# Text softmax of a cross-attention layer: exponentials taken per head from PSUM, with the row sums alongside

## The chip, the core and the metric

The kernel runs on one core of a Trainium2 chip. A core has TensorE (PE, matrix products, with its weight loads PEld), VectorE (DVE), ScalarE (ACT), GpSimd (POOL) and SyncE (SP, which issues DMAs here). Each engine works through its own queue in order; semaphores tie the queues together. Working data lie in SBUF; TensorE writes to eight PSUM banks, from which VectorE and ScalarE read. The metric is the device time of one execution in microseconds, the median of several runs.

## The reference, cut to what matters

Two batches, 2048 image tokens of width 640, 128 context tokens of width 384, of which the last four are adapter tokens; 8 heads of 80. "The text" is the attention over the first 124 context tokens:

```python
query = hidden_states @ Wq
keyt = enc @ Wk          # 124 text tokens
valt = enc @ Wv
hs = _mha(query, keyt, valt)
# _mha, per head:
scores = einsum('bhqd,bhkd->bhqk', qh, kh) * d ** -0.5
probs = softmax(scores, axis=-1)
out = einsum('bhqk,bhkd->bhqd', probs, vh)
# adapter part: ca_q1 from the four adapter tokens attends over all of hidden_states,
# its result, through Wq, attends over the four tokens -> ca_hs2
out = (hs + ca_hs2) @ Wout + b_out + residual
```

All is float32.

## The kernel before

The program is written out by hand for TensorE: every matmul and transposition is recorded in the order in which the Python generators yield it, and TensorE keeps that order. VectorE, ScalarE and GpSimd take what the recording layer gives them, in order too; `dve.behind` adds order on VectorE without a wait. Line 28 is the helper through which all matmuls go, line 41 that of the transpositions, line 55 that of all VectorE instructions.

**The text.** `scores(m)` (line 971) works on unit m, two tiles of 128 query rows. For each tile and each half u of four heads, six matmuls put 4 x 124 scores into one PSUM bank `sc` (128 x 496). VectorE takes the maximum of each head (`m`, 128 x 4, line 993) and writes scores less maximum into the SBUF tile `e` (in the profile `p`, lines 994 to 997), which ends the bank's use. When both halves are there, one ScalarE instruction takes the exponential of all 8 heads in place (line 999, 128 x 992). `divided` (line 1007) sums each head on VectorE (`r`, line 1012), takes the reciprocal, and has GpSimd multiply the probabilities by it (line 1014); it is called one tile later. `turned_out` (line 1031) transposes both tiles in 32 x 32 blocks on VectorE (`eb`) and sends them to HBM (`kept`); `turned` (line 1017) reads them back as `pT`; `values` (line 1056) multiplies them by the values (`ph`), copies the result to SBUF (`hsT`, by ScalarE or VectorE in turn), multiplies by the output weights (`po`) and adds the residual rows `xo` on VectorE. The pool of `e` has two buffers, that of `m` and `r` three.

**The adapter.** `maxima` (line 792) computes scores `s` of the adapter's queries against image rows, four banks at a time, and has VectorE take their maxima (`mx`, 128 x 2048). `contraction` (line 825) computes them again row by row: four matmuls write `s` (the four banks of `q4`, one buffer), ScalarE takes the exponential into `ea` (line 856, 128 x 1536), and the products with it are accumulated in `acc`. In TensorE's order the scores of step st+1 stand behind the products of step st-1 and a stretch of text work, and they need the four banks that `ea` of step st has read. At the end of each half `accs` (line 863) is copied by ScalarE.

**The order.** `weave` and `Mix` lay the text between the steps of the adapter: first all of batch 0's maxima, beside them the queries `pq`; then batch 0's contraction (in the profile from about 154 to 290 us) with text units 0 to 4; batch 1's maxima (to about 462 us) with units 5 to 8; batch 1's contraction (to about 592 us) with units 9 to 11; and then the rest of the text alone. Until then four of the eight banks belong to the adapter's scores and one to its accumulation (batch 1's maxima lend that one out), so that the text, the queries and the outputs share three or four; after that all eight.

Of the kernel before, what the change touches and what calls it, by code (L numbers as in the profile page):

```python
# [8 lines left out]
F32 = mybir.dt.float32  # L9
AF = mybir.ActivationFunctionType  # L10
ALU = mybir.AluOpType
AX = mybir.AxisListType

P = 128
HEADS = 8
# [4 lines left out]
class TensorInOrder:  # L20
# [6 lines left out]
    def matmul(self, out, lhsT, rhs, **kw):  # L27
        ins = self.tc.nc.tensor.matmul(out, lhsT, rhs, **kw)  # L28
        self.tc.keep_in_program_order(ins)
        n = 1  # L30
        for size in rhs.shape[1:]:
            n *= size
        if min(lhsT.shape[0], lhsT.shape[1]) <= 32:
            self.us += (n / 1.2 + 97) / 2e3
        elif min(lhsT.shape[0], lhsT.shape[1]) <= 64:
            self.us += (n / 1.2 + 54) / 1e3
        else:
            self.us += 2 * max(n / 1.2, 109) / 1e3
# [139 lines left out]
def kernel(  # L178
# [39 lines left out]
    nc = tc.nc  # L218
    pe = TensorInOrder(tc)
    dve = VectorBehind(tc)  # L220
    B, S, H = x.shape
    NTOK, CAD = enc.shape[1], enc.shape[2]
    NK = NTOK - T
# [6 lines left out]
    SCALE = float(D) ** -0.5  # L230
# [28 lines left out]
    def mm_tile(name, pool=None):  # L259
        if pool is None:  # L260
            pool = ps_turns[ps_turn[0] % len(ps_turns)]
            ps_turn[0] += 1
        return pool.tile([P, 512], F32, tag="mm", name=name)
# [72 lines left out]
    small = ctx.enter_context(tc.tile_pool(name="small", bufs=3))  # L336
# [629 lines left out]
    def tiles(m):  # L966

        b, m = divmod(m, NST // 2)
        return [(b, 2 * m + k) for k in range(2)]

    def scores(m):

        q = q_of[m // 2]
        before = None
        for b, st in tiles(m):
            rows = slice(st % 4 * P, (st % 4 + 1) * P)
            e = pools["e"].tile([P, HEADS, NTOK], F32, tag="e", name=f"p_{b}_{st}")
            for u in range(2):
                sc = mm_tile(f"sc_{b}_{st}_{u}")
                for i, c in enumerate((2 * u, 2 * u + 1, 4)):  # L980
                    to = sc[:, : 4 * NK].rearrange("p (i j k) -> p i j k", i=2, j=2)
                    n0 = 2 * c if c < 4 else 2 * (4 + u)
                    matmul(
                        to[:, i, :, :] if c < 4 else to[:, :, 1, :],
                        q[:, c, rows],
                        kpad[:, b, n0 : n0 + 2, :],
                        start=(i == 0),
                        stop=(i == 2),
                        skip_group_check=True,
                    )  # L990
                s4 = sc[:, : 4 * NK].rearrange("p (h k) -> p h k", k=NK)
                m = small.tile([P, 4], F32, tag="m", name=f"m_{b}_{st}_{u}")
                dve.tensor_reduce(m, s4, AX.X, ALU.max)
                dve.tensor_tensor(
                    e[:, 4 * u : 4 * u + 4, :NK], s4,
                    m.unsqueeze(2).to_broadcast([P, 4, NK]), ALU.subtract,
                )
                yield
            nc.scalar.activation(e[:, :, :NK], e[:, :, :NK], AF.Exp, scale=SCALE)  # L999
            nc.gpsimd.memset(e[:, :, NK:], 0.0)  # L1000
            if before is not None:
                divided(*before)
            before = b, st, e
        yield
        divided(*before)

    def divided(b, st, e):

        last = dve.last
        et = e[:, :, :NK]  # L1010
        r = small.tile([P, HEADS], F32, tag="r", name=f"r_{b}_{st}")
        dve.behind(dve.tensor_reduce(r, et, AX.X, ALU.add), last)
        dve.reciprocal(r, r)
        nc.gpsimd.tensor_tensor(et, et, r.unsqueeze(2).to_broadcast([P, HEADS, NK]), ALU.mult)  # L1014
        e_of[b, st] = e

# [174 lines left out]
    def ahead(m):  # L1191

        parts, needs, more = [], [], []
        if m + 1 < units:
            more = [turned(m + 1, 1 if m + 2 == units else 3), residual(m + 1)]
        more.append(completed())
        if m + 2 < units:
            parts.append(stage(("s", m + 2), scores(m + 2)))  # L1200
        if m + 3 == units:
            parts.append(out_soon(m + 2))
        n = m // 2 + 2
        if NSB <= n < len(blocks):
            if m % 2 == 0:
                parts.insert(0, room(n))
                parts.append(queries(n, (0, 1, 2)))
                needs += [("again", *blocks[n]), slots.free(1)]
            else:
                parts.append(stage(("q", *blocks[n]), queries(n, (3, 4))))  # L1210
        return stage(("t", m), unit(m, more, parts), *needs)
# [56 lines left out]
    for sb in range(NSB):  # L1268
# [6 lines left out]
    open_late()  # L1275
    first = chain(
        stage(("s", 0), scores(0)),
        together(turned(0, 1), stage(("s", 1), scores(1)), residual(0)),
    )
    text.parts[:] = [beside(first, chain(*text.parts), 2), *[ahead(m) for m in range(units)]]  # L1280
# [68 lines left out]
```

## Time and profile before

| | us |
|---|---|
| median of 3 runs (lowest, highest) | 747.44 (747.37, 749.98) |
| the profiled execution | 744.53 |
| its span, first to last instruction | 742.8 |
| VectorE, row sums `r`, 32 of 1,165 ns | 37.3 |
| VectorE, maxima `m`, 64 of 666 ns | 42.3 |
| GpSimd, products by the reciprocals, 32 of 1,964 ns | 61.2 |

Times in the profile's groups are busy time, mean ns of one instruction, and then the idle time of the engine just ahead of the group, with what ended it. "x64" is the number of instructions. In a timeline the first two columns are start and duration in us, counted from the span's start; the bracket says how long the engine had been idle and what released it. TensorE's granted clock was full (1.00) in every stretch of this execution.

By stage, TensorE was busy for 142.4 of the first 149.9 us, 135.9 of the 140.1 us to 290.0, 170.4 of the 172.0 us to 462.0, 134.0 of the 135.0 us to 597.0 and 142.4 of the last 145.8 us. VectorE was busy for 77, 66, 123, 45 and 65 us of these stretches, ScalarE for 31, 56, 32, 57 and 17 us.

### The profile page before, as it was taken

To read this page: it belongs to the slowest core of one execution; us is meant where nothing else is said; L and a number is where in the kernel's file an instruction comes from. 1 tells how busy PE (TensorE), PEld (TensorE's weight loads), DVE (VectorE), ACT (ScalarE), POOL (GpSimd) and SP (SyncE) were. 2 spreads that over 40 slices of the span, in tenths; PEclk is the share of its full clock that TensorE was granted. 3 is DMA by queue.
4 is the path that set the end of the run, shared out by engine and by line. 5 is a ranking of instruction groups with operands and counts; after the bars stand their busy time and mean duration, and the time that the engine had idled before them with its cause. 6 is when DMAs were issued, how large, how long until landed. Compare 5 with 4: busy or idle time off the path is not lost.

```text
span 742.8 us, 9398 instructions
## 1 busy us (share of the span) xinstructions
PE 725.1 (98%) x3809; PEld 371.3 (50%) x3809; DVE 376.3 (51%) x507; ACT 193.4 (26%) x239; POOL 133.1 (18%) x184
## 2 busy tenths in 40 slices
PE   7999999999989999999999999999999999999998
PEld 4543433343444446555445454444433556566765
DVE  2155746544274537678768585412330546346631
ACT  2221121033444342212021110543434411011100
POOL 7000000002021013225311221010010012631330
PEclk9999999999999999999999999999999999999999
DMA  9927240004734867599988294500910426985793
GB/s 291 176 36 126 34 38 1 0 1 115 106 119 71 200 97 177 133 261 225 226 167 215 36 198 111 147 20 19 190 49 19 136 84 201 232 218 157 213 247 95
DMA packets 147429, 96.28 MB, mean 130 GB/s; under 512 B 118133, under 2 KB 118965, under 8 KB 145338
## 3 DMA queue, kind: packets, MB, share of 16 engines
q1 hardware_dynamic: 142266, 85.10, 48.1%
q0 software_dynamic: 5120, 10.59, 8.1%
q8 instruction: 30, 0.49, 0.3%
q14 instruction: 13, 0.11, 0.1%
HBM read 63.81 MB, written 31.85 MB: 129 GB/s over the span
## 4 chain that ended last, share of the span: by engine, by line
PE 92%; DVE 4%; issue 1%; ACT 1%; DMA 0%; POOL 0%; DVEq 0%; ACTq 0%; POOLq 0%
PE po L28 24%; PE pq L28 24%; PE s L28 13%; PE sc L28 11%; PE acc L28 6%; PE ph L28 5%; PE pyz L28 3%; PE pk L28 1%; PE pv L28 1%; PE pt_y L41 1%; DVE m L55 1%; DVE p L55 1%; ACT ea L856 1%; DVE xt L55 1%; DVE mx L55 0%
## 5 line engine op out<-in xcount | busy, mean ns | idle before, releaser
L28 PE MATMUL po<-wout_sb,hsT 128*128 128x320 f32 x640 | 186.6, 438 | 0.8 <-DVE xo L55 0.6
L28 PEld LDWEIGHTS po<-wout_sb,hsT 128*128 128x128 f32 x640 | 118.4, 190 | 70.1 <-issue 25.1
L28 PE MATMUL pq<-xt,wq_sb 128*128 128x512 f32 x320 | 151.4, 605 | 0.0
L55 DVE TENSOR_REDUCE mx<-s 128x4 f32<-128x2048 f32 x48 | 109.9, 2290 | 65.9 <-PE s L28 65.9
L856 ACT ACTIVATE ea<-s 128x1536 f32<-128x1536 f32 x64 | 92.7, 1448 | 111.4 <-PE s L28 111.3
L1014 POOL TENSOR_TENSOR p<-p,r 128x992 f32<-128x992 f32 x32 | 61.2, 1964 | 263.4 <-DVE r L55 263.3
L55 DVE TENSOR_TENSOR xo<-xo,po 128x320 f32<-128x320 f32 x64 | 30.9, 483 | 141.0 <-PE po L28 140.6
L28 PE MATMUL sc<-kpad,q 128*128 128x248 f32 x384 | 94.1, 384 | 0.9 <-DVE p L55 0.9
L28 PEld LDWEIGHTS pq<-xt,wq_sb 128*128 128x128 f32 x320 | 57.2, 189 | 74.3 <-issue 68.6
L28 PEld LDWEIGHTS sc<-kpad,q 128*128 128x128 f32 x384 | 69.2, 189 | 33.7 <-issue 18.1
L55 DVE TENSOR_REDUCE m<-sc 128x4 f32<-128x496 f32 x64 | 42.3, 666 | 53.8 <-PE sc L28 53.8
L28 PE MATMUL s<-ca,yz 32*128 32x384 f32 x512 | 59.4, 533 | 2.3 <-ACT ea L856 2.3
L272 ACT COPY q<-pq 128x512 f32<-128x512 f32 x29 | 17.0, 585 | 166.0 <-PE pq L28 166.0
L999 ACT ACTIVATE p<-p 128x992 f32<-128x992 f32 x32 | 33.0, 1030 | 93.2 <-DVE p L55 93.2
L28 PE MATMUL s<-yz,ca 32*128 32x512 f32 x384 | 54.7, 640 | 1.8 <-DVE mx L55 1.0
L1109 POOL DMA_INDIRECT xo<-o,query x24 | 37.4, 1557 | 100.3 <-DMA xo<-in_x_dram 50.6
L28 PE MATMUL acc<-ea,y_sb 128*32 128x384 f32 x512 | 54.5, 498 | 0.2 <-ACT ea L856 0.2
L28 PE MATMUL ph<-pT,vpad 128*32 128x256 f32 (+1 forms) x512 | 50.0, 387 | 1.8 <-DVE hsT L55 1.8
L55 DVE TENSOR_TENSOR p<-sc,m 128x496 f32<-128x496 f32 x64 | 42.6, 670 | 1.7
L55 DVE STREAM_TRANSPOSE eb<-p 128x1024 f32<-128x1024 f32 x32 | 38.1, 1222 | 3.6 <-POOL p L1014 3.6
L28 PE MATMUL pq<-xt,wq 128*128 128x512 f32 x80 | 38.3, 603 | 0.0
L55 DVE TENSOR_REDUCE r<-p 128x8 f32<-128x992 f32 (+1 forms) x34 | 37.7, 1111 | 0.0
(142 smaller groups left out, 390.6 us busy)
## 6 DMA issues: line engine op xcount, KB each, us to landing
kept<-eb SPq DMA_DIRECT2D x16, 1024.0 KB, 5.3
pT<-kept SPq DMA_DIRECT2D x64, 256.0 KB, 6.0
xi<-in_x_dram SPq DMA_DIRECT2D x44, 256.0 KB, 5.1
xo<-in_x_dram SPq DMA_DIRECT2D x32, 320.0 KB, 4.8
out_dram<-xo SPq DMA_DIRECT2D x22, 320.0 KB, 3.2
xi<-in_x_dram SPq DMA_DIRECT2D x44, 64.0 KB, 4.7
early<-xo SPq DMA_DIRECT2D x8, 320.0 KB, 2.6
xe<-early SPq DMA_DIRECT2D x8, 320.0 KB, 6.0
```

The source lines that it names most:

```text
L28: ins = self.tc.nc.tensor.matmul(out, lhsT, rhs, **kw)
L41: ins = self.tc.nc.tensor.transpose(out, in_, ident)
L55: self.last = getattr(self.tc.nc.vector, name)(*args, **kw).ins
L272: nc.scalar.copy(dst, src)
L856: nc.scalar.activation(e, q4[:, :, :CAD], AF.Exp, scale=SCALE)
L999: nc.scalar.activation(e[:, :, :NK], e[:, :, :NK], AF.Exp, scale=SCALE)
L1014: nc.gpsimd.tensor_tensor(et, et, r.unsqueeze(2).to_broadcast([P, HEADS, NK]), ALU.mult)
L1109: nc.gpsimd.indirect_dma_start(out=t, out_offset=None, in_=o2_of[b], in_offset=bass.IndirectOffsetOnAxis(ap=query[:, st : st + 1], axis=0) ...
```

## The change

The subtraction of the maxima and the row sums leave VectorE. VectorE multiplies the four maxima of a half by minus the scale, in place (128 x 4). ScalarE then takes the exponentials straight from the PSUM bank, one instruction for each head (128 x 124), with the scaled maximum as its bias and the row's sum as a second output, written into a column of `r`, which is now made in `scores`. The instruction over all heads goes, and so does the row sum in `divided`, which keeps the reciprocal. TensorE's and SyncE's orders stay the same instruction for instruction.

```diff
             e = pools["e"].tile([P, HEADS, NTOK], F32, tag="e", name=f"p_{b}_{st}")
+            r = small.tile([P, HEADS], F32, tag="r", name=f"r_{b}_{st}")
...
                 dve.tensor_reduce(m, s4, AX.X, ALU.max)
-                dve.tensor_tensor(
-                    e[:, 4 * u : 4 * u + 4, :NK], s4,
-                    m.unsqueeze(2).to_broadcast([P, 4, NK]), ALU.subtract,
-                )
+                dve.tensor_scalar(m, m, -SCALE, None, ALU.mult)
+                for i in range(4):
+                    h = 4 * u + i
+                    nc.scalar.activation(
+                        e[:, h, :NK], s4[:, i, :], AF.Exp, bias=m[:, i : i + 1], scale=SCALE,
+                        accum_out=r[:, h : h + 1],
+                    )
                 yield
-            nc.scalar.activation(e[:, :, :NK], e[:, :, :NK], AF.Exp, scale=SCALE)
             nc.gpsimd.memset(e[:, :, NK:], 0.0)
...
-    def divided(b, st, e):
+    def divided(b, st, e, r):
         last = dve.last
+        dve.behind(dve.reciprocal(r, r), last)
         et = e[:, :, :NK]
-        r = small.tile([P, HEADS], F32, tag="r", name=f"r_{b}_{st}")
-        dve.behind(dve.tensor_reduce(r, et, AX.X, ALU.add), last)
-        dve.reciprocal(r, r)
         nc.gpsimd.tensor_tensor(et, et, r.unsqueeze(2).to_broadcast([P, HEADS, NK]), ALU.mult)
```

## The prediction

> **What bounds the kernel now.** I read the busy shares and the chain of waits first, then the groups by form, then the timeline of the two contractions.
>
> ```profile
> PE 725.1 (98%) x3809; PEld 371.3 (50%) x3809; DVE 376.3 (51%) x507; ACT 193.4 (26%) x239; POOL 133.1 (18%) x184
> PE 92%; DVE 4%; issue 1%; ACT 1%; DMA 0%; POOL 0%; DVEq 0%; ACTq 0%; POOLq 0%
> ```
>
> TensorE sets the time: busy for 725.1 of 742.8 us. Of the 17.7 us left, 4.35 pass before its first instruction and about 3 at the end, so no relief of another engine can bring more than some 10 us, and a microsecond by which TensorE waits longer is a microsecond of the result.
>
> ```profile
> L999 ACT ACTIVATE p<-p 128x992 f32<-128x992 f32 x32 | 33.0, 1030 | 93.2 <-DVE p L55 93.2
> L856 ACT ACTIVATE ea<-s 128x1536 f32<-128x1536 f32 x64 | 92.7, 1448 | 111.4 <-PE s L28 111.3
> L775 ACT ACTIVATE yz<-pyz,ones 128x512 f32<-128x512 f32 x16 | 10.1, 683 | 31.9 <-PE pyz L28 31.9
> L272 ACT COPY q<-pq 128x512 f32<-128x512 f32 x29 | 17.0, 585 | 166.0 <-PE pq L28 166.0
> L272 ACT COPY vca<-pvca 128x128 f32<-128x128 f32 x1 | 0.3, 265 | 0.4 <-PE pvca L28 0.4
> L272 ACT COPY vpad<-pv 124x32 f32<-124x32 f32 x8 | 1.1, 199 | 0.0
> L55 DVE TENSOR_TENSOR p<-sc,m 128x496 f32<-128x496 f32 x64 | 42.6, 670 | 1.7
> L55 DVE RECIPROCAL r<-r 128x8 f32<-128x8 f32 x32 | 6.4, 201 | 0.9
> ```
>
> These rows price what goes and what comes. The next, from the timeline of batch 0's contraction, shows where ScalarE reaches TensorE:
>
> ```profile
> 247.35 0.93 PE L28 MATMUL s<-ca,yz 32*128 32x384 f32 x8
> 247.46 0.67 DVE L55 TENSOR_REDUCE m<-sc 128x4 f32<-128x496 f32 x1 [0.73 <-PE sc L28]
> 248.17 0.67 DVE L55 TENSOR_TENSOR p<-sc,m 128x496 f32<-128x496 f32 x1
> 248.94 1.03 ACT L999 ACTIVATE p<-p 128x992 f32<-128x992 f32 x1 [3.19 <-DVE p L55]
> 249.87 1.43 ACT L856 ACTIVATE ea<-s 128x1536 f32<-128x1536 f32 x1
> 251.36 0.93 PE L28 MATMUL s<-ca,yz 32*128 32x384 f32 x8 [1.28 <-ACT ea L856]
> ```
>
> The last sc group ends at 247.35, where s begins. From there a chain runs over the maximum, the subtraction, the text's exponential and, behind it in ScalarE's queue, ea; the next s needs ea's four banks. The chain is 4.01 us long here and TensorE stands idle for 1.28. It existed only for the second half of a tile; behind a first half ea followed s at once. One place of that kind, in batch 1's contraction:
>
> ```profile
> 577.75 2.36 DVE L55 STREAM_TRANSPOSE eb<-p 128x1024 f32<-128x1024 f32 x2
> 578.29 0.93 PE L28 MATMUL s<-ca,yz 32*128 32x384 f32 x8
> 579.34 1.45 ACT L856 ACTIVATE ea<-s 128x1536 f32<-128x1536 f32 x1 [3.36 <-PE s L28]
> 580.03 0.64 DVE L55 TENSOR_REDUCE m<-sc 128x4 f32<-128x496 f32 x1
> 580.94 0.93 PE L28 MATMUL s<-ca,yz 32*128 32x384 f32 x8
> ```
>
> Here VectorE is busy with the transpositions when the scores of 578.29 are ready, the maximum is 1.63 us late (580.03 against 578.40), and nobody cares: ea has not waited for it, and the next s stands 2.65 us behind the last.
>
> **VectorE's side.** It loses 64 subtractions (64 x 0.670 = 42.6 us) and 32 row sums (32 x 1.165 = 37.3 us), and gains 64 small multiplications of 128x4. Nearest row: the reciprocal of 128x8, 0.20 us, so 12.8 us. 67 us less, but VectorE is no bound: the places where TensorE visibly waits for its work, at 213.27 (1.84 us) and 345.94 (0.87), are all that can come back. As bounds for one multiplication I take 0.15 (the reduction of 128x4 to 128x1 at 8.20 us) and 1.83 us: in the first 12 us of the timeline eight multiplications of 128x16 and 128x4, from SBUF to SBUF, show 0.97 to 1.83 us, all of them ending at 11.3 to 11.4 us, while GpSimd runs fills from 9.62 to 11.27.
>
> The Trainium skill has a rule for this, SBUF — State Buffer, section Who interferes with whom: a VectorE instruction in a two-port mode, which a multiplication with all operands in SBUF can enter, and a GpSimd instruction lock each other out for a whole instruction. That rule speaks against the change, since the subtraction it replaces read PSUM. By it each multiplication that meets a GpSimd product would take up to 1.96 us; by the reciprocal's row, 0.20.
>
> I take 0.20: in the contractions GpSimd is busy for only 4.4 of the 80 us from 460, and its products come ahead of the transpositions, not beside the maxima. I charge the long one in the upper bound alone, at 345 us, where a GpSimd gather starts at 345.09 for 1.54 us.
>
> **ScalarE's side.** It loses 32 x 1.030 = 33.0 us and gains 256 exponentials of 128x124 with a bias column and a sum. Without both, a copy of 128x128 out of PSUM takes 0.265 us; the bias column costs 683 - 585 = 0.098; together 0.363. Instructions that follow each other overlap by 0.10 (two y_sb copies of 0.589 last 1.07), so one head adds 0.263. The sum's price stands in no row. Lower bound nothing: it is formed as the elements pass. Upper bound 0.30: if a second small instruction has to deliver it, nearest row the 124x32 copy of 0.199 us, unable to start before the first has drained, so that the 0.10 overlap is lost as well. I take the middle, 0.15: a step of 0.413 (bounds 0.263 and 0.563), 1.65 us for four heads (1.05 to 2.25). ScalarE then carries 193 - 33 + 256 x 0.413 = 266 us, 36%: on average no bound.
>
> The Trainium skill's page ScalarE: Activation LUTs, section What ACT_TABLE_LOAD costs, gives about 280 ns plus 0.833 per element for an ACTIVATE with a bias column and 93 ns of overlap back to back: 290 ns for a head, without the sum; by that figure the four heads would take 1.16 us instead of the 1.05 of the rows. Its fixed price per instruction speaks against cutting one instruction of 992 elements into eight.
>
> **The path.** The new chain from the end of a sc group to the next possible s: 0.11 to the maximum, 0.67, 0.04 gap, 0.20 multiplication, 0.10 to ScalarE, the four heads, 1.43 ea, 0.05 = 2.60 + 1.65 = 4.25 us (3.65; 4.85). The same sum for the old second half (0.67 for the multiplication, 0.94 for the heads) gives the 4.01 seen. What is new is that *both* halves have it. ea is queued behind the heads, and s and the accumulation wait for ea. Going through the two contractions, with the distance from the sc group's end to the next s before (each value: middle; lower; upper):
> - 158.68 to 161.77 (3.09 us): +1.16; 0.56; 1.76. 201.07 to 204.17 (3.10): +1.15; 0.55; 1.75. Behind 180.8 and 191.9 lie 4.41 us: 0; 0; 0.44 each.
> - 204 to 215: the row sums (1.17 and 1.13 us) stood ahead of GpSimd's products, these ahead of the transpositions, and these ahead of the idle 1.84. GpSimd now starts sooner, but its second product waits for the heads, and the next ea behind heads that wait for the transpositions. s of 214.29 comes some 0.8 earlier: -0.84; -1.0; -0.2.
> - 243.24: the maximum is 1.44 late behind eb (244.79); 4.25 + 1.44 against 4.11 = 1.58, of which the following pair with its 1.28 of idle time gives back 0.91: +0.67; -0.3; 1.9.
> - Four halves in a row, 466.25 to 482.43, 3.96 to 4.11 us apart: each second one is late, since a late s also makes the next sc late; less the 0.48 of idle time at 481.9: +0.39; -0.36; 1.6. 527.15 to 534.79: +0.36; -0.3; 1.3.
> - 578.29: 4.25 + 1.63 against 2.65 = +3.23; 2.63; 3.83. The largest single term.
> - 590.26: accs now stands behind four heads, and the transposition at 591.15 waits for it: +0.60; 0; 1.2.
>
> In batch 1's maxima ea doesn't run, but a bank is held until the last head has read it. At 345.94 TensorE waited for the bank of the scores whose subtraction ended at 345.79; the heads end at 345.09 + 0.34 + 1.65 = 347.08: +1.3; 0.7; 1.9, and 1.4 more if the multiplication waits for GpSimd. At 433.12 about +0.3; 0; 1.0. After 597 us eight banks are there and ScalarE is busy for 17 of 146 us: nothing. The last transpositions end at 710.6 and their pT is asked for at 716.7, behind other DMAs of SP's queue; without row sums on VectorE the heads' 3.3 us fit in before that. If they didn't, the last ph group (725.5) would be late. `r` and `m` now live longer, until GpSimd's product and the last head; each has three buffers and at most two are in use at those times, so nothing; with fewer, the maximum of a later half would wait for the heads.
>
> Sum: 1.16 + 1.15 - 0.84 + 0.67 + 0.39 + 0.36 + 3.23 + 0.60 + 1.6 = +8.3 us; lower +2.5; upper +18.3. Against the profiled 744.53: 752.8. The median of the runs lies 2.91 above that execution, so the forecast is 747.44 + 8.3 = 755.7 us.
>
> **The rivals.** (A) The sum is free and the heads overlap fully (0.263 a head): the lower sum, 749.9. For it: ScalarE's rows differ only by elements and bias. Against: a second output has to be written by something. (B) Each head is drained before its sum is written (0.563): 765.7. For it: 256 small outputs; against: no such wait in any row. (C) Faster: relief of VectorE decides. Its place is the idle time behind VectorE and behind ea after a subtraction: 1.84 + 1.28 + 0.87 + 0.48 + 0.48 = 4.95 us, so 742.5. It decides if the heads cost less than subtraction and exponential did, 2.60 + 4 x step below 4.01, with margin, step under 0.25, and if the late maxima at 244.79 and 580.03 did not reach ea. The second condition speaks strongly against it: ScalarE's order puts those heads ahead of ea.
>
> **How the numbers follow.** Forecast (step 0.35 to 0.5) 0.57, A 0.18, B 0.18, C 0.05, something unseen 0.02. The change of this kernel that a measurement can tell from none is about 0.5%, 3.7 us. A falls to both sides of it, mostly within: slower 0.80, same 0.15, faster 0.05. The range leaves out C, the bottom of A and the top of B: 749 to 764.
>
> **What would show it.** Right: rows of 128x124 at 0.36 us with a step near 0.41; ScalarE near 266 us and VectorE near 309; an idle TensorE of about 3 us at the s behind the scores of 578; ea released by text exponentials. Wrong: TensorE's busy share unchanged (A), or idle time at every s of the contractions (B); multiplications of 128x4 well over 0.2 us throughout; a late pT at the end. The step's length is what most decides the size.

## The result, and the profile after

| us | before | after |
|---|---|---|
| median (lowest, highest) | 747.37 (745.29, 749.98), 7 runs | 752.72 (751.90, 753.66), 7 runs |
| the profiled execution | 744.53 | 753.52 |
| its span | 742.8 | 751.8 |
| its mean granted clock | 1.000 | 0.995 |

The ratio is 1.0082 with a 95% interval of 1.0061 to 1.0102: 0.8% slower, 5.35 us between the medians, 3.0 us less than forecast. The first view is again that of the busy shares and of the chain of waits.

```profile
PE 729.1 (97%) x3809; PEld 372.6 (50%) x3809; DVE 308.4 (41%) x475; ACT 251.9 (34%) x719; POOL 133.6 (18%) x184
...
PE 91%; DVE 4%; ACT 3%; issue 1%; DMA 1%; POOL 0%; SPq 0%; DVEq 0%; ACTq 0%
```

VectorE lost 68 us of work and TensorE is still busy for 97% of the span; among the engines' shares of the chain only ScalarE's rose, from 1 to 3%. The groups by form show what VectorE and ScalarE do now:

```profile
L998 ACT ACTIVATE p<-sc,m 128x124 f32<-128x124 f32 x256 | 89.7, 368 | 96.1 <-DVE m L55 89.0 <-PE ph L28 7.1
L998 ACT ACTIVATION_READ_ACCUMULATOR p<-sc,m 128x1 f32 x256 | 53.4, 209 | 0.0
L55 DVE TENSOR_SCALAR m<-m 128x4 f32<-128x4 f32 x64 | 10.6, 167 | 1.7
```

The second output is an instruction of its own, 0.209 us long. What a head really takes is not to be had by adding the two means; it is read from the distance of the starts, in the timeline of the chain that starts at 203.74 us (at 201.07 before the change):

```profile
203.74 0.93 PE L28 MATMUL s<-ca,yz 32*128 32x384 f32 x8
203.85 0.67 DVE L55 TENSOR_REDUCE m<-sc 128x4 f32<-128x496 f32 x1 [0.56 <-PE sc L28]
204.56 0.17 DVE L55 TENSOR_SCALAR m<-m 128x4 f32<-128x4 f32 x1
...
204.84 0.36 ACT L998 ACTIVATE p<-sc,m 128x124 f32<-128x124 f32 x1 [3.41 <-DVE m L55]
205.10 0.19 ACT L998 ACTIVATION_READ_ACCUMULATOR p<-sc,m 128x1 f32 x1
205.20 0.36 ACT L998 ACTIVATE p<-sc,m 128x124 f32<-128x124 f32 x1
...
206.22 1.46 ACT L856 ACTIVATE ea<-s 128x1536 f32<-128x1536 f32 x1
...
207.73 0.93 PE L28 MATMUL s<-ca,yz 32*128 32x384 f32 x8 [0.83 <-ACT ea L856]
```

The read-out starts at 205.10, before the exponential's 0.36 us are over, and the next head at 205.20, before the read-out ends. Four heads take 206.22 - 204.84 = 1.38 us, 0.345 each, and the chain from the scores' end to the next s 207.73 - 203.74 = 3.99 us. The place that the forecast called the largest, after:

```profile
579.95 1.42 PE L28 MATMUL sc<-kpad,q 128*128 128x248 f32 x6
581.29 0.93 PE L28 MATMUL s<-ca,yz 32*128 32x384 f32 x8
...
583.04 0.64 DVE L55 TENSOR_REDUCE m<-sc 128x4 f32<-128x496 f32 x1
...
584.00 0.36 ACT L998 ACTIVATE p<-sc,m 128x124 f32<-128x124 f32 x1 [5.01 <-DVE m L55]
...
585.37 1.46 ACT L856 ACTIVATE ea<-s 128x1536 f32<-128x1536 f32 x1
...
586.88 1.66 PE L28 MATMUL s<-ca,yz 32*128 32x384 f32 x8 [2.87 <-ACT ea L856]
588.48 1.51 PE L28 MATMUL acc<-ea,y_sb 128*32 128x384 f32 x8
```

The maximum is late behind `eb` as before, but now ea stands behind the four heads that wait for it: ea starts at 585.37 instead of at some 582.3 (1.05 behind its s, as before), and TensorE is idle for 2.87 us. Then something happens that no step of the forecast holds: s takes 1.66 us instead of 0.93, and the accumulation 1.51 instead of 0.85. The stretches of 5 us show why (columns: length; busy time and number of instructions of PE, PEld, DVE, ACT and POOL; TensorE's granted clock; DMA share; GB/s):

```profile
580.00:585.00 5.00, 4.02 (x31) 1.85 (x29) 3.70 (x5) 1.00 (x6) 0.25 (x2) 1.00 0.23 95
585.00:590.00 5.00, 3.12 (x17) 0.80 (x17) 0.00 (x0) 3.63 (x7) 0.00 (x0) 0.59 0.78 246
590.00:595.00 5.00, 5.00 (x30) 2.71 (x30) 1.54 (x3) 1.35 (x8) 0.00 (x0) 0.73 0.00 0
```

The missing share, 0.41 x 5 + 0.27 x 5 = 3.4 us, is 6.8 us at half clock, and inside the span the trace's clock records have exactly one such piece, 6.83 us from 585.9 on.

Where the time went is seen when each of the 3809 matmuls is set against itself in the trace of before (their order is the same): the steps of that delay, measured from the first matmul of each.

| place (us before) | forecast: middle (lower; upper) | step in the trace |
|---|---|---|
| first 12 us | not named | +1.4 |
| 153 | not named | +0.61 |
| 158.68 to 161.77 | +1.16 (0.56; 1.76) | +0.88 |
| 201.07 to 204.17 | +1.15 (0.55; 1.75) | +0.90 |
| 204 to 218 | -0.84 (-1.0; -0.2) | -1.91 + 0.82 - 0.22 = -1.31 |
| 243.24 to 251.4 | +0.67 (-0.3; 1.9) | +1.28 - 1.28 = 0 |
| 290 | not named | -0.42 |
| 345.94; 433.12 | +1.3 (0.7; 1.9); +0.3 (0; 1.0) | +1.04; +0.07 |
| 466 to 482 | +0.39 (-0.36; 1.6) | +0.03 |
| 527 to 535 | +0.36 (-0.3; 1.3) | +0.35 - 0.32 = +0.03 |
| 578.29 | +3.23 (2.63; 3.83) | +2.94 |
| half clock behind it | not named | +2.7 |
| 590 | +0.60 (0; 1.2) | +0.34 |
| sum | +8.3 | +9.25 |

The sum is that of the two profiled executions (spans 9.0 apart, the first matmul 0.25 earlier; smaller steps elsewhere are not listed). Without the start, 7.85; without the half clock too, 5.1.

### The profile page after: what moved, and what is told of

Read it like the earlier page. It is cut to its first block, busy times and chain, and to the rows that moved or that the text cites. A ratio compares the mean times of both kernels' runs of the same rounds, so it can differ in the third digit from the quotient of the medians.

```text
span 751.8 us, 9853 instructions
## 1 busy us (share of the span) xinstructions
PE 729.1 (97%) x3809; PEld 372.6 (50%) x3809; DVE 308.4 (41%) x475; ACT 251.9 (34%) x719; POOL 133.6 (18%) x184
## 4 chain that ended last, share of the span: by engine, by line
PE 91%; DVE 4%; ACT 3%; issue 1%; DMA 1%; POOL 0%; SPq 0%; DVEq 0%; ACTq 0%
PE po L28 24%; PE pq L28 23%; PE s L28 13%; PE sc L28 11%; PE acc L28 6%; PE ph L28 6%; PE pyz L28 3%; ACT p L998 2%; ACT ea L856 1%; PE pk L28 1%; PE pv L28 1%; PE pt_y L41 1%; DVE m L55 1%; DVE eb L55 1%; DVE xt L55 1%
## 5 line engine op out<-in xcount | busy, mean ns | idle before, releaser
L998 ACT ACTIVATE p<-sc,m 128x124 f32<-128x124 f32 x256 | 89.7, 368 | 96.1 <-DVE m L55 89.0
L998 ACT ACTIVATION_READ_ACCUMULATOR p<-sc,m 128x1 f32 x256 | 53.4, 209 | 0.0
L28 PEld LDWEIGHTS s<-ca,yz 32*128 32x128 f32 x512 | 20.2, 184 | 40.4 <-issue 23.0
```

The source lines that it names most:

```text
L998: nc.scalar.activation(e[:, h, :NK], s4[:, i, :], AF.Exp, bias=m[:, i : i + 1], scale=SCALE, accum_out=r[:, h : h + 1],)
```

## The experiments

Theory 1: the loss is what stands ahead of ea in ScalarE's queue. The heads wait for a maximum that VectorE delivers late, ea waits behind them, and s waits for ea. Rival 1: the form is the price, 256 instructions with a read-out each. Rival 2: the PSUM banks that the heads hold longer. Rival 3: the half clock comes by itself and has nothing to do with idle time. Each ratio is to the kernel before on the same chip in the same job (medians 746.1 to 746.6 us of 17 to 32 runs). "Old form" is subtraction and row sum on VectorE and one exponential of eight heads.

**The old form in one tile of 32.** The tile is the one at 579 us.

```diff
+                if (b, st) == (1, 6):
+                    dve.tensor_tensor(
+                        e[:, 4 * u : 4 * u + 4, :NK], s4,
+                        m.unsqueeze(2).to_broadcast([P, 4, NK]), ALU.subtract,
+                    )
+                    yield
+                    continue
...
+            if (b, st) == (1, 6):
+                nc.scalar.activation(e[:, :, :NK], e[:, :, :NK], AF.Exp, scale=SCALE)
```

> The changed kernel with the old form (subtraction on VectorE, one exponential of eight heads, row sum on VectorE) in one tile of 32, the tile of batch 1 whose first half's scores end at 578 us before. Theory 1 with a clock that falls because TensorE stood idle: the 2.9 us of waiting there go, and so does the stretch at half clock behind it (1.5 to 3.5 us): about 747.3 us, clock 1.00. Rival 3 (the half clock comes from something else): only the wait goes, about 749.8 us, clock still 0.995 to 0.998. Rival 1 (the price is the 256 small instructions): 8 of 256 go, 752.5 us.

Measured: 749.65 us (747.81 to 753.81, 12 runs), ratio 1.0037 (1.0016 to 1.0057). The step of 2.94 is gone from the trace, and no half clock follows there. The mean clock, 0.995 to 0.998 in all seven runs of the changed kernel, is 1.000 in nine of these twelve. By the clock rival 3 falls, though the median alone stands nearer to its number than to theory 1's. The profiled execution has a half clock of 3.41 us at another place, 354 us, behind an idle stretch of 1.87 us there: idle time elsewhere can bring it too. One tile also changes several things at once, so the next run changes one.

**One half later.** Only the four heads of the half at 579.95 are moved, one step down in the recording and behind that step's ea; their form stays.

```diff
                 dve.tensor_scalar(m, m, -SCALE, None, ALU.mult)
+                if (b, st, u) == (1, 6, 0):
+                    yield
                 for i in range(4):
...
+                    if (b, st, u) == (1, 6, 0):
+                        act_behind(ins, ea_last[0])
-                yield
+                if (b, st, u) != (1, 6, 0):
+                    yield
```

`act_behind` adds order on ScalarE without a wait; `ea_last` is the last ea recorded.

> The changed kernel with one edit at one place: the four heads of the half whose scores end at 581.3 us (tile 6 of batch 1, first half) are recorded one step later and stand behind that step's ea on ScalarE; the form stays the new one, all other heads stay where the change put them. Theory 1 (the place in the queue makes the 2.9 us there, and the half clock follows the idle time): that step and its half clock go, 3.5 to 5 us below the changed kernel, ratio to before 1.001 to 1.005, near the kernel with the old form in that one tile (1.0037), with a clock of 0.999 to 1.000 in most runs. Rival 1 (the form, its 256 instructions and sums, is the price): less than 1 us below the changed kernel, ratio 1.007 to 1.008. Rival 3 (the half clock has nothing to do with this place): 2.9 us below, but the clock stays at 0.995 to 0.998.

Measured: 748.1 us (747.48 to 753.44, 12 runs), ratio 1.0022 (0.9998 to 1.0047), clock 1.000 in nine of twelve. The timeline of this kernel at the same place:

```profile
581.41 0.93 PE L28 MATMUL s<-ca,yz 32*128 32x384 f32 x8
...
582.46 1.45 ACT L862 ACTIVATE ea<-s 128x1536 f32<-128x1536 f32 x1 [3.36 <-PE s L28]
584.06 0.93 PE L28 MATMUL s<-ca,yz 32*128 32x384 f32 x8
...
585.12 1.45 ACT L862 ACTIVATE ea<-s 128x1536 f32<-128x1536 f32 x1 [0.35 <-PE s L28]
...
586.46 0.36 ACT L1006 ACTIVATE p<-sc,m 128x124 f32<-128x124 f32 x1
```

ea starts at 582.46 instead of 585.37, the next s follows 2.65 us behind the last as before the change, and the same four heads run at 586.46 without holding anybody up. All other steps of the table are there as they were. Of the 256 instructions, the place of four decided over half of the loss: theory 1, against rivals 1 and 3.

**All heads later.** The same edit for every half.

```diff
                 dve.tensor_scalar(m, m, -SCALE, None, ALU.mult)
+                yield
                 for i in range(4):
...
+                    if ea_last[0] is not None:
+                        act_behind(ins, ea_last[0])
-                yield
```

> The changed kernel with the four heads of each half recorded one step later and placed on ScalarE behind the ea that was recorded last, nothing else moved. Theory 1: ea follows its scores at once, TensorE's idle time behind ea (7.4 us in the changed kernel, 2.3 before) goes to under 0.5 us, no half clock; the bank at 346 still costs about 1 us: 743 to 745 us, faster than both. Rival 1 (price of the instructions): 752 us as changed. Rival 2 (what counts is how long the heads hold their PSUM banks): the banks are held 1.5 to 3 us longer still, so above 753 us.

Measured: 743.65 us (743.18 to 749.10, 9 runs), ratio 0.9958 (0.9943 to 0.9973): faster than before, with the same 256 heads and read-outs. The waits of s for ea (us in total, number, longest), first in the kernel before, then after the change:

```profile
PE s L28 <- ACT ea L856: 2.3, 3, 1.3
PE s L28 <- ACT ea L856: 7.4, 8, 2.9
```

Here none is left. What stays of the change's steps is +0.61 at 153, +1.04 at 346 and +0.07 at 433; gains are 1.09 at 213, 0.42 at 290, and 1.57, 0.56 and 0.56 at the places where the kernel before itself waited for ea. The profiled execution, the slowest of the nine, has a slow start (+5.5) and a half clock of 3.41 us behind the wait at 346 besides.

**The old exponential later.** Is that gain VectorE's relief? The kernel before, with its one exponential, which is recorded a step behind its scores already, put behind the last recorded ea on ScalarE in the same way:

```diff
-            nc.scalar.activation(e[:, :, :NK], e[:, :, :NK], AF.Exp, scale=SCALE)
+            ins = nc.scalar.activation(e[:, :, :NK], e[:, :, :NK], AF.Exp, scale=SCALE).ins
+            if ea_last[0] is not None:
+                act_behind(ins, ea_last[0])
```

> The kernel before, with its one exponential of eight heads recorded one step later and placed on ScalarE behind the last recorded ea. Theory 1 (what counts is what stands ahead of ea in ScalarE's queue): the three places of before where TensorE stood idle behind ea after a text exponential (1.28 us at 250, 0.48 at 482, 0.48 at 535) close, no new one opens, so some 2 us below before, ratio 0.995 to 0.998, near the kernel with the heads later. Rival (the gain of the heads placed later came from VectorE's relief, the place in the queue only undid the loss): ratio 1.000, and the kernel with the heads later stays clearly below this one.

Measured: 741.39 us (740.41 to 745.03, 9 runs), ratio 0.9921 (0.9893 to 0.9949). The rival named there falls. Theory 1's size was too small: besides the three places (steps -1.57, -0.56, -0.56) the idle 1.84 us at 213 go as well (-1.91), because on VectorE the maximum and the copy `hsT`, for which TensorE waited there, now stand ahead of the transpositions, which wait for GpSimd's products. First the kernel before, then this one:

```profile
210.81 1.25 DVE L55 STREAM_TRANSPOSE eb<-p 128x1024 f32<-128x1024 f32 x1 [0.56 <-POOL p L1014]
...
212.54 0.67 DVE L55 COPY hsT<-ph 128x512 f32<-128x512 f32 x1
...
213.27 1.08 PE L28 MATMUL ph<-pT,vpad 128*64 128x256 f32 x8 [1.84 <-DVE hsT L55]
```

```profile
209.26 0.68 DVE L55 COPY hsT<-ph 128x512 f32<-128x512 f32 x1
...
209.96 1.19 DVE L55 STREAM_TRANSPOSE eb<-p 128x1024 f32<-128x1024 f32 x1
...
211.57 1.08 PE L28 MATMUL ph<-pT,vpad 128*64 128x256 f32 x8
```

The stretch of the second contraction in this kernel has no idle TensorE at all, with VectorE busier than after the change (46.29 us against 30.71):

```profile
462.00:600.00 138.00, 138.00 (x851) 63.11 (x851) 46.29 (x77) 57.37 (x52) 11.70 (x11) 1.00 0.33 81
```

So the order on ScalarE gains with either form, and the new form gains nothing beyond it here: by these steps, -4.6 us with the old exponential later, -2.5 with the heads later.

**Heads later, old form in batch 1's maxima.** For the eight tiles there, as in the first diff with another condition.

> The heads one step later and behind ea, as in the kernel with the heads later, but the old form (subtraction on VectorE, one exponential, row sum on VectorE) for the eight tiles whose softmax lies in batch 1's maxima. Theory 1: the wait for the bank at 346 us shrinks by 0.9 us and that at 433 by 0.3, so 0.5 to 1.3 us below the kernel with the heads later: 742.3 to 743.2 against 743.65 there, ratio to before 0.994 to 0.9955. Rival (the banks are not what that wait is for): the same time as the kernel with the heads later.

Measured: 741.93 us (741.30 to 746.02, 12 runs), ratio 0.9940 (0.9917 to 0.9964). The step at 346 and the small one at 433 are gone: those two belong to the banks that the heads hold, which is all that is left of rival 2. The step at 153, +0.61, is not one of these tiles and stays.

**The sum left out.** ScalarE writes no second output; the row sums go back to VectorE, everything else as changed.

```diff
-                        accum_out=r[:, h : h + 1],
...
-        dve.behind(dve.reciprocal(r, r), last)
+        dve.behind(dve.tensor_reduce(r, et, AX.X, ALU.add), last)
+        dve.reciprocal(r, r)
```

> The changed kernel without the second output: the heads' exponentials keep their bias column, the row sums are VectorE's again (32 of 1.17 us). Theory 1 (the heads stand ahead of ea in ScalarE's queue, and s waits for ea): a head's step falls from 0.345 us to about 0.26, the chain from the scores to the next s from 3.99 to about 3.66 us, so the late s at 161 and 204 cost 0.57 us each instead of 0.9, the one behind 578 about 2.6 instead of 2.94; the return of the row sums gives back most of the 1.9 us won at 213. Total about 751 to 752.5 us, so still slower than before. Rival 1 (the read-out of the sum is what costs): within 0.3% of before, 747 to 749 us.

Measured: 753.02 us (750.66 to 759.67, 6 runs), ratio 1.0080 (1.0055 to 1.0105). The heads are shorter, in the timeline of this kernel:

```profile
209.64 1.13 ACT L998 ACTIVATE p<-sc,m 128x124 f32<-128x124 f32 x4 [3.41 <-DVE m L55]
210.64 1.47 ACT L856 ACTIVATE ea<-s 128x1536 f32<-128x1536 f32 x1
```

Four heads take 1.00 us instead of 1.38, so the sum costs 0.095 us a head. The steps shrink accordingly (0.51 at 161.8, 0.53 at 204, 2.57 at 581), but the total doesn't: near 213 TensorE is idle for 0.86 and 1.57 us (1.84 before, 0.76 after the change), with a half clock of 6.83 us that begins there, and the one behind 581 lasts 3.41. The sum isn't where the loss lies: against rival 1. By the figures of the Trainium skill, ScalarE: Activation LUTs, section What ACT_TABLE_LOAD costs, an estimate is about 383 ns for such a head without the sum and 290 ns back to back; here the row was 367 ns and the step 250.

**The new form only outside the contractions.** Old form for `(b == 0 and st < 10) or (b == 1 and 2 <= st < 8)`.

> The change only in tiles whose softmax lies outside the two contractions (batch 1's maxima and the last stage, 12 units of 16 tiles in part: 16 tiles of 32); the old form for the tiles in the contractions. Theory 1: no heads stand ahead of an ea, so of the delays only the bank at 346 us (+0.9) and that at 433 (+0.3) stay: 0.5 to 1.5 us above before, ratio 1.000 to 1.002. Rival 1 (every head costs time wherever it stands): half of the loss, 2.5 to 4 us, ratio 1.0035 to 1.005. Rival 2 (banks held longer are the loss): most of the 5 to 6 us, since the banks held by heads are only where no ea shares ScalarE.

Measured: 749.3 us (745.84 to 755.76, 12 runs), ratio 1.0024 (0.9994 to 1.0053). The interval holds theory 1's numbers and rival 1's, so the time alone decides nothing. The trace does for that one execution: of the change's steps only those in batch 1's maxima are there (+1.03 at 346, +0.06 at 433), beside a slow start (+7.2 by 13 us) and a half clock of 3.41 us behind the old wait at 218 us. A step of 0.62 at 725 is there as well, but the kernel before with one copy (below) has the same, 0.61.

**A wait put into the kernel before.** To part idle time from its cause, copies of step 13's scores (128x1536, 1.45 us each) stand ahead of the ea at 579 us in the kernel before; no head is involved.

```diff
+                waits = []
+                if (b, j, st) == (1, 1, 13):
+                    for _ in range(2):
+                        waits.append(nc.scalar.copy(..., q4[:, :, :CAD]).ins)
                 ins = nc.scalar.activation(e, q4[:, :, :CAD], AF.Exp, scale=SCALE).ins
+                for other in waits:
+                    act_behind(ins, other)
```

Two copies:

> The kernel before, with two ScalarE copies of that step's scores (128x1536, 1.45 us each, into a stretch of SBUF that is no longer read) ahead of the one ea at 579 us. It holds the next s up by about 2.7 us and changes nothing else. If the half clock follows from the idle time: 2.7 us plus 1.5 to 3.5 us, so 751.5 to 753.5 us and a clock of 0.995 to 0.998. Rival 3 (it has another cause): 750 us, clock 1.00.

One copy:

> The kernel before with one ScalarE copy of 128x1536 ahead of the ea at 579 us, so that the s behind it comes about 1.2 us late instead of 2.7. If the half clock follows only a long idle stretch of TensorE, this costs 1.2 to 1.4 us (ratio 1.0015 to 1.002) and the clock stays at the one of before; if any idle microsecond there brings it, 2.5 to 4 us with a clock of 0.995 to 0.998; if the half clock has nothing to do with idle time, the same clock as before in most runs.

Four copies:

> The kernel before with four ScalarE copies of 128x1536 ahead of the ea at 579 us: the s behind it comes 5.3 to 5.6 us late (by one copy: 1.33; by two: 2.65). If the half clock follows a long idle stretch, every run has a lower mean clock (0.995 or below where two pieces of 3.41 us come, since each costs 1.7 us of full clock in 745, that is 0.0023) and the loss is 5.3 plus 1.4 to 2.8 us: ratio 1.0085 to 1.011. If it has nothing to do with the idle time, the clock is that of before, and the ratio 1.007 to 1.0075.

| copies | median us (lowest, highest; runs) | ratio (interval) | idle at the next s | runs with a clock under 0.999 |
|---|---|---|---|---|
| one | 747.46 (746.13, 750.49; 12) | 1.0002 (0.9977, 1.0028) | 1.11 | 2 of 12 |
| two | 753.83 (751.28, 754.65; 6) | 1.0088 (1.0066, 1.0111) | 2.59 | 4 of 6 |
| four | 754.29 (753.74, 758.62; 6) | 1.0107 (1.0067, 1.0146) | 5.89 | 6 of 6 |

With four copies, the line of the late s and the stretches behind it:

```profile
588.31 1.66 PE L28 MATMUL s<-ca,yz 32*128 32x384 f32 x8 [5.89 <-ACT ea L868]
```

```profile
585.00:590.00 5.00, 1.69 (x12) 0.62 (x16) 0.00 (x0) 3.22 (x3) 0.00 (x0) 0.69 0.45 157
590.00:595.00 5.00, 5.00 (x25) 2.46 (x26) 0.89 (x2) 1.45 (x1) 0.00 (x0) 0.62 0.00 0
```

An s stretched to 1.66 us, as after the change, with no head near. The longer TensorE stands idle, the more executions have the half clock: rival 3 falls. In the profiled execution with two copies it did not come, although TensorE was idle for 2.59 us; the last section says what parted the two. The times of the runs with two copies are not fully accounted for: their median lies 7.7 us above before's 746.12, while the step at the late s is 2.66 in the trace and 6.83 us at half clock cost at most 3.4 more. By 13 us the profiled execution is 7.2 us behind before's; how the other five started is not on record.

## Why the prediction was right, and where its numbers were off

**Right: the mechanism and the largest place.** ea queued behind heads that wait for a late maximum was the forecast's main step, and +2.94 at 578 answers to its +3.23. With the measured chain of 3.99 its own sum gives 3.99 + 1.63 - 2.65 = 2.97, and 0.90 and 0.89 at the first two places, against 0.88 and 0.90 seen. Behind a first half nothing had been lost before; that is why the loss is new.

**Luck: the sum.** The places that the forecast names came to +4.9 us in the trace instead of +8.3; most of the terms were too large. What it doesn't name, the half clock (+2.7) and the later start (+1.4) above all, brings the two profiled executions to 9.25 apart. That the sum of the forecast comes near this is luck.

**Mis-sized: the step of a head.** Taken at 0.413, measured 0.345. The sum cost 0.095 and not 0.15, and the head without it 0.25 and not 0.263. Both lie inside the bounds; that is 0.27 us too much at each place, and ScalarE at 251.9 instead of 266 us.

**Mis-sized: where one wait pays for another.** At 243, 466 and 527 the forecast left +0.67, +0.39 and +0.36 net; the trace shows 0, +0.03 and +0.03. At 243 the following pair gave back its whole 1.28, not the 0.91 assumed. From 204 to 218 the gain was 1.31, beyond the bound of 1.0.

**Missing: the clock.** Every term counted an idle microsecond as one microsecond. Behind the largest stretch the matmuls ran at half clock, and that cost 2.7 us more, nearly as much as the stretch itself. The profile of before, with a full clock from 7.33 us on, could not show it. Missing as well: the 0.61 us at 153, where the next scores wait for the second subtraction of `ca`. The profile puts that wait down to `ca`; why the bank that they take comes free only there was not tried.

**Failed: the way from the execution to the median.** The forecast added before's 2.91 us between profile and median to the changed kernel. Its profiled execution lies 0.80 above its own median, so the places, 8.3 forecast and 7.85 with the clock, became 5.35 between medians. Executions differ in the start-up by up to 7 us (last section), but which share of the difference of medians that makes was not measured; it stays open.

**VectorE.** 308.4 us against 309 forecast; a multiplication took 0.167 against 0.20. The rule on VectorE and GpSimd locking each other out (the Trainium skill, SBUF — State Buffer, section Who interferes with whom) was charged in the upper bound at 345 us. There a multiplication of 0.171 us, at 346.95, ran while a gather and two fills of GpSimd were under way: no lock showed. By this trace none of the 64 multiplications met a GpSimd product, so what such a meeting costs is not shown.

**The rivals.** The free sum (A) falls with the read-out at 0.095 us, the drained head (B) with a step of 0.345 against its 0.563. C named the right condition, that the late maxima must not reach ea: where the queue meets it, the kernel is indeed faster than before. But the old form gains no less there (0.9921 against 0.9958), so the gain isn't VectorE's relief, which C named as its source.

## What to carry to other kernels

Before moving work onto an engine that has room on average, ask what stands behind it in that engine's queue, and how late its input comes: a short instruction that waits holds up a long one that everybody needs. Put it behind that instruction; here this turned 0.8% of loss into 0.4% of gain, and the same reordering without the change gave 0.8%. And idle time of TensorE can cost more than its length once some 2 us of it come together: here 2.9 us cost 5.7.

## What the runs showed of the hardware

**The clock looks at pieces of 3.41 us.** Half-clock stretches in the traces, leaving out their last microseconds, last 3.41 or 6.83 us, and begin a whole number of 3.413 us after the moment when the clock first became full (after the change 9.06 us; 585.9 is 169 pieces later). Cutting the traces, up to the same point, into these pieces and adding up TensorE's idle time in each: up to 1.81 us in a piece with full clock, no half clock followed; at 1.83 to 1.84 it followed once in four; from 1.87 on (1.87, 1.88, 1.89, 1.90, 2.50, 3.41) six times in six. The 2.59 us behind two copies fell 1.29 and 1.29 into two pieces, and the clock stayed full, while the 2.87 us after the change fell 1.89 and 0.98. So the same idle stretch is cheap or dear by where it falls. These are readings of eleven profiled executions and the kernel before's; no run set the phase. The Trainium skill, TensorE: Matmul & The Clock Gate, section What's actually happening, has a free-running window of 3413 ns, which the pieces agree with, and lets the clock fall after at least one idle window; here 1.87 us of idle time in a window were enough, and the measurement decides.

**The start differs between executions of one program.** The clock became full at 7.33 us in before's profile and at up to 19.6 us in others. The stretch of 15 to 20 us, first before, then the kernel with the new form outside the contractions:

```profile
15.00:20.00 5.00, 5.00 (x13) 2.14 (x12) 0.75 (x3) 0.00 (x0) 0.00 (x0) 1.00 1.21 300
```

```profile
15.00:20.00 5.00, 5.00 (x8) 2.05 (x7) 1.20 (x4) 0.00 (x0) 0.00 (x0) 1.00 1.14 323
```

TensorE is busy throughout in both, with 13 matmuls against 8: these run at the slow clock (the same products start 0.85 us apart instead of 0.43), although the column still says 1.00 ahead of the first clock record. By 13 us the second execution is 7.2 us behind. Not all of this is the clock: ahead of these stretches TensorE waited 1.75 us for the DMA of image rows `xz` and 0.61 us for VectorE's `x_last`, waits that the profile of before doesn't have.

**An output of sums is a second instruction.** Its row shows 0.209 us, but most of that overlaps its neighbours: 0.095 us is what it added to a head.
